# Four heads to a unit in the grouped-query layer of a cross-attention stack

## The chip, the core and the metric

The kernel runs on one core of a Trainium2 chip. TensorE (PE) multiplies matrices and writes to PSUM, which has eight banks of 512 fp32 columns on 128 partitions; VectorE (DVE), ScalarE (ACT) and GpSimd (POOL) do the rest, and SyncE (SP) issues most transfers between DRAM and on-chip memory. The engines run side by side, each through its own queue in order, and wait for each other on semaphores. The metric is the device time of one execution in microseconds (us); the time before is a median over runs, and the traces come from one further, profiled execution.

## The reference

Four attention layers transform `x` (2048 queries of 256 values) against one context of 1601 tokens of 512 values. Layers 0, 2 and 3 are alike: 16 heads of 64 values, with a bias of -20 times a mask on the columns of a few named tokens. Layer 1, the second one, is the subject here: 16 query heads of 16 values share four key and value heads, and `x` is normalized first.

```python
# masked layers (three of them)
logits = einsum('bhqd,bhkd->bhqk', q, k) * 64 ** -0.5 + col_bias
out = einsum('bhqk,bhkd->bhqd', softmax(logits), v)
x = out @ Wo + bo + x
# second layer
inv = rsqrt(mean(x * x, axis=-1) + 1e-5)
xn = x * inv * norm_w
q = (xn @ wq).reshape(B, T, 16, 16)       # query heads 4g .. 4g+3 belong to group g
k = (cond @ wk).reshape(B, S, 4, 16)
v = (cond @ wv).reshape(B, S, 4, 16)
scores = einsum('btgrd,bsgd->bgrts', qg, k) * 16 ** -0.5
x = x + einsum('bgrts,bsgd->btgrd', softmax(scores), v).reshape(B, T, 256) @ wo
```

## The kernel before

The queries are cut into four sets of 512 (`b`), the 1601 keys into 13 chunks of 128 (the last of 65). `x` stays on the chip, transposed, in `xs`. A *block* is a pair of heads of a masked layer, or a group of four query heads of the second. A *unit* is one set of queries with one pair of heads: 32 units for each masked layer (8 blocks, 4 sets), and 32 for the second layer (4 blocks, 4 sets, two pairs per group, the list `SUBS`).

One loop (L1052) writes the order of all work. A *step* handles one chunk of three units at once: the scores of one unit (`ca`), the exponentials of a unit 17 steps behind (13 chunks and `DELAY` 4) and the values of a unit one step further behind (`LAG` 1). The engines' orders are pinned to what this loop writes (L1107 to L1113), except that GpSimd and the transfers are not.

In a masked unit, `masked_scores` multiplies two heads on 64 partitions each in fp32 (L755), ScalarE copies the scores to SBUF (L767), and VectorE keeps a running maximum over the keys (L772). After 13 steps the maximum is transposed, reduced and spread over all partitions through DRAM (`maxima`, `on_all_partitions`, `maxima_spread`). Then VectorE subtracts it (L837), ScalarE takes the exponential (L844), GpSimd adds up the chunks for the denominators (L849), and PE multiplies by the values, two heads on 64 columns each (L872).

In a unit of the second layer, `split` has cut the 16 values of each query and key into three bf16 parts, and `stack` has laid eight products of parts along the 128 contraction rows (`q8`, `k8`); a ninth product lies apart (`k9`, `max_rows`). Row maxima come from one bf16 matmul per head with 512 keys (`grouped_scores`, L788), reduced by VectorE straight from PSUM (L793); the negated maxima are cut into three parts, transposed (L828) and copied into three rows of `max_rows` (L831). The input of the exponentials is computed by two more matmuls per head (L853 and L858), the second of which subtracts the maximum, and ScalarE takes the exponential from PSUM (L862). The values carry a column of ones, so that the denominators come out as a row of the result (`denominators`, L900).

What fills the gaps are *pieces*: projections of keys, values and queries, denominators, output projections. Each has a cost, and is written at the end of a step when its due step has come or when the step's credit allows it (`Pieces.step`). Most of them write the one PSUM bank `pm`. The other banks: two buffers of two banks for scores (`ps_s`), one buffer of two for the spread maxima of masked units (`ps_b`, which the second layer also uses for scores), and one bank for the values' result.

Before the second layer starts, `normalize` (L654) computes the root mean square of each set of queries with ones as weights, divides `x` by it on VectorE and stores the normalized `x` in DRAM; the keys of the second layer are projected and split chunk by chunk (`keys`, L524) during the last block of the first layer.

Of the kernel before, what the change touches and what calls it, by code (L numbers as in the profile page):

```python
# [18 lines left out]
P = 128  # L19
QB = 512  # L20
# [13 lines left out]
def tile_cross_attention_stack(ctx: ExitStack, tc: tile.TileContext, t: dict, out: bass.AP):  # L34
# [23 lines left out]

    nc = tc.nc
# [15 lines left out]
    NP = 19  # L75
# [7 lines left out]
    ps_s = ctx.enter_context(tc.tile_pool(name="ps_s", bufs=2, space=PSUM))  # L83
    ps_b = ctx.enter_context(tc.tile_pool(name="ps_b", bufs=1, space=PSUM))
# [6 lines left out]
    nc.vector.memset(ones, 1.0)  # L91

# [117 lines left out]
    def first_context_slice(i):  # L210
# [3 lines left out]
        for c in range(4 * i, min(4 * i + 4, NT)):  # L214
# [6 lines left out]
            pt = ps_s.tile([P, NCT, P], FP, name="s")  # L221
# [14 lines left out]
    MX, RA, RB, RE = 0, 3, 6, 9  # L236
    HALVES = (0, 64)
    max_keys = const.tile([P, P], BF, name="max_keys")
    tail_keys = [const.tile([P, NTAIL], BF, name=f"tail_keys{l}") for l in range(NL)]
    max_cols = const.tile([P, QT, P], FP, name="max_cols")  # L240
# [14 lines left out]
    def token_rows():  # L255
# [6 lines left out]
        nc.gpsimd.memset(max_cols, 0.0)  # L262
# [4 lines left out]
        row_of = small.tile([P, 3], FP, name="row_of", bufs=1)  # L267
        for j, (r0, r1) in enumerate(((MX, RA), (RA, RB), (RB, RE))):
            for h in HALVES:
                nc.vector.tensor_reduce(  # L270
                    row_of[h : h + 64, j : j + 1], ident[h : h + 64, h + r0 : h + r1], AX.X, ALU.add
                )
        for b in range(NB):
            for h in HALVES:
                nc.vector.tensor_copy(
                    max_cols[:, :, h + RA : h + RE],
                    parts[:, :, b * QT : (b + 1) * QT].rearrange("p r q -> p q r"),
                )
            pt = ps_m.tile([P, QT, P], FP, name="pm")
            for q in range(QT):  # L280
                nc.tensor.transpose(pt[:, q, :], max_cols[:, q, :], ident)
            nc.vector.tensor_copy(bias_rows[:, ts(b, QB)], pt.rearrange("p a b -> p (a b)"))
        nc.gpsimd.memset(max_cols, 0.0)
        nc.vector.memset(max_keys, 0.0)
        for h in HALVES:
            nc.vector.memset(max_keys[h : h + RA, :], 1.0)
        for l in range(NL):
# [3 lines left out]
            for to, j in ((0, 0), (1, 2)):  # L291
# [11 lines left out]
            nc.vector.tensor_scalar(tail_keys[l], only, row_of[:, 1:2], row_of[:, 0:1], ALU.mult, ALU.add)  # L303
            nc.vector.scalar_tensor_tensor(
                tail_keys[l], marks[:, 1, :], row_of[:, 2:3], tail_keys[l], ALU.mult, ALU.add
# [13 lines left out]
    den_rows = const.tile([P, 2], FP, name="den_rows")  # L319
    one_row = const.tile([P, 1], FP, name="one_row")  # L320
    nc.gpsimd.memset(one_row, 0.0)
    for h, r in enumerate(HALVES):
        nc.gpsimd.tensor_copy(den_rows[:, h : h + 1], ident[:, r + 16 : r + 17])
        nc.gpsimd.memset(one_row[r : r + RA, :], 1.0)
# [5 lines left out]
    class Masked:  # L330
# [25 lines left out]

        def wo(self, u, sub):
            return u.wo
# [34 lines left out]
        def query_pieces(self, unit):  # L393
# [4 lines left out]
            def queries(j):  # L398
                if j == 0:
                    unit.q = heads.tile([P, QB], FP, name="q")  # L400
# [10 lines left out]
    class Grouped:  # L411
# [3 lines left out]

        BLOCKS, HEADS = 4, 2
        SUBS = [(0, 1), (2, 3)]
        name = "L1_xattn_"
        OWN = 32
        ka = vs = None
        Q_PARTS = (0, 0, 0, 1, 1, 1, 2, 2)  # L430
        K_PARTS = (0, 1, 2, 0, 1, 2, 0, 1)

        def stackers(self, kind, parts):

            both = [const.tile([P, 4, 8, 16], BF, name=f"{kind}{x}") for x in "ab"]
            for x in both:
                nc.gpsimd.memset(x, 0.0)
            for j, part in enumerate(parts):
                half = 0 if part == 0 else 64
                nc.gpsimd.tensor_copy(  # L440
                    both[part // 2][:, :, j, :],
                    ident[:, half : half + 64].rearrange("p (h d) -> p h d", d=16),
                )
            return both

        def load(self, n):
# [3 lines left out]
            if n == 0:  # L450
                self.sel_q = self.stackers("sel_q", self.Q_PARTS)
                self.sel_k = self.stackers("sel_k", self.K_PARTS)
                self.last_q = const.tile([P, 2, P], BF, name="last_q")
                self.last_k = const.tile([P, 4, P], BF, name="last_k")
                nc.gpsimd.memset(self.last_q, 0.0)
                nc.gpsimd.memset(self.last_k, 0.0)
                for h, r in enumerate(HALVES):
                    to = slice(r + self.OWN, r + self.OWN + 16)
                    for i in range(2):
                        j = 64 + 16 * self.SUBS[i][h]  # L460
                        nc.gpsimd.tensor_copy(self.last_q[:, i, to], ident[:, j : j + 16])
                    for g in range(4):
                        j = 64 + 16 * g
                        nc.gpsimd.tensor_copy(self.last_k[:, g, to], ident[:, j : j + 16])
                self.wk = weights.tile([P, NCT, 2, 64], FP, name="wk", bufs=1)
                self.wv = weights.tile([P, NCT, 64], FP, name="wv", bufs=1)
                for half in range(2):
                    nc.sync.dma_start(
                        out=self.wk[:, :, half, :],
                        in_=t[self.name + "wk"].rearrange("(k p) f -> p k f", p=P),  # L470
                    )
                nc.sync.dma_start(
                    out=self.wv, in_=t[self.name + "wv"].rearrange("(k p) f -> p k f", p=P)
                )
            u.wq = weights.tile([P, NC, 2, 64], FP, name="wq")
            for half in range(2):
                nc.sync.dma_start(
                    out=u.wq[:, :, half, :],
                    in_=t[self.name + "wq"][:, ts(n, 64)].rearrange("(k p) f -> p k f", p=P),
                )  # L480
            return u

        def load_wo(self, u):
            u.wo_of = weights.tile([P, 2, C], FP, name="wo")
            nc.gpsimd.memset(u.wo_of, 0.0)
            for i in range(2):
                for h, r in enumerate(HALVES):
                    j = 64 * u.n + 16 * self.SUBS[i][h]
                    nc.sync.dma_start(
                        out=u.wo_of[r : r + 16, i, :], in_=t[self.name + "wo"][j : j + 16, :]  # L490
                    )

        def wo(self, u, sub):
            return u.wo_of[:, sub, :]

        def split(self, src, a, b, scale):

            top = slice(64, P)
            nc.scalar.mul(a, src, scale)
            rest = work.tile([P, 512], FP, name="rest", bufs=1)  # L500
            less = rest[top, : src.shape[1]]
            nc.vector.scalar_tensor_tensor(
                less, src[top], scale, a[top], ALU.mult, ALU.subtract
            )
            nc.vector.tensor_copy(a[top], less)
            nc.vector.tensor_tensor(b[top], less, a[top], ALU.subtract)

        def stack(self, dst, sel, j, a, b):
            n = a.shape[1]
            ps = ps_m.tile([P, 512], FP, name="pm")  # L510
            nc.tensor.matmul(
                ps[:, :n], sel[0][:, j].rearrange("p t d -> p (t d)"), a, start=True, stop=False
            )
            nc.tensor.matmul(
                ps[:, :n], sel[1][64:, j].rearrange("p t d -> p (t d)"), b[64:],
                start=False, stop=True,
            )
            nc.vector.tensor_copy(dst, ps[:, :n])

        def projections(self, u):  # L520
            if u.n:
                return None

            def keys(c, ct):  # L524
                if self.ka is None:
                    self.ka = heads.tile([P, T], BF, name="ka", bufs=1)
                    self.kb = heads.tile([P, T], BF, name="kb", bufs=1)
                a, m = TCH[c]
                pk = ps_m.tile([P, QB], FP, name="pm")[:, :m]
                for k in range(NCT):  # L530
                    nc.tensor.matmul(
                        pk, self.wk[:, k].rearrange("p h d -> p (h d)"), ct(k)[:, :m],
                        start=(k == 0), stop=(k == NCT - 1),
                    )
                self.split(pk, self.ka[:, a : a + m], self.kb[:, a : a + m], 1.0)
# [14 lines left out]
        def own_keys(self, u):  # L550


            def begin():
                u.kT = heads.tile([P, T], FP, name="kT")
                both = u.kT[:, :].bitcast(BF)
                u.k8, u.k9 = both[:, :T], both[:, T:]

            def stacked(a, n):
                if u.kT is None:
                    begin()  # L560
                self.stack(
                    u.k8[:, a : a + n], self.sel_k, u.n, self.ka[:, a : a + n],
                    self.kb[:, a : a + n],
                )

            def last(a, n):
                ps = ps_m.tile([P, 512], FP, name="pm")
                nc.tensor.matmul(
                    ps[:, :n], self.last_k[64:, u.n, :], self.kb[64:, a : a + n],
                    start=True, stop=True,  # L570
                )
                nc.scalar.activation(
                    u.k9[:, a : a + n], ps[:, :n], AF.Identity, bias=one_row
                )

            found = []
            for a, n in TBK:
# [569 lines left out]
```

## Time and profile before

| | us |
|---|---|
| median of 3 runs (5645.54 to 5646.53) | 5646.52 |
| the profiled execution | 5638.94 |
| its span, first to last instruction | 5637.2 |
| PE busy in the span | 5255.5 (93%) |
| VectorE busy | 3981.3 (71%) |
| ScalarE busy | 3346.0 (59%) |
| GpSimd busy | 3018.6 (54%) |
| first exponential of the second layer, from the span's start | 1582.3 |
| its last exponential | 2903.6 |

A line of the profile names the source line, the engine, the operation, and what is written from what (`s<-q,kT`) with partitions and columns; "x4" merges four records, and an fp32 matmul leaves two records, each with its own weight load (PEld). "Idle before" is how long the engine had waited, with what ended it. Of two successive lines on PE the difference of the starts is what the first one costs, since records overlap at their ends. The three masked layers lie before and behind the second one; the granted TensorE clock is a share of full speed.

### The profile page before, as it was taken

How to read it: one execution, taken by the hardware profiler on the slowest of the kernel's cores; microseconds unless marked ns; L12 is line 12 of the kernel's file. 1: busy time of each engine (PE TensorE's matmuls, PEld its weight loads, DVE VectorE, ACT ScalarE, POOL GpSimd, SP SyncE). 2: the span in 40 equal slices, each digit the busy share in tenths (PEclk: the TensorE clock that was granted, in tenths of full speed). 3: DMA queues.
4: the chain of work that ended last, by engine and by line, in shares of the span. 5: the costliest groups of instructions: out<-in, count | busy, mean ns of one | idle time of the engine just before them, and what ended most of it. 6: DMA issues, size and time to landing. Idle time of an engine off the chain costs nothing.

```text
span 5637.2 us, 63697 instructions
## 1 busy us (share of the span) xinstructions
PE 5255.5 (93%) x23412; PEld 2070.8 (37%) x23412; DVE 3981.3 (71%) x4183; ACT 3346.0 (59%) x4096; POOL 3018.6 (54%) x1476
## 2 busy tenths in 40 slices
PE   6899999998889999999999999999999999999997
PEld 4333433343322333233334334333334333334332
DVE  3777777778765555555557777777777777777786
ACT  2666666665533333333356667666667666667675
POOL 1677777775520000000026777777777777777777
PEclk8999999999889999999999999999999999999998
DMA  4222222222100000001112222222222222222211
GB/s 122 63 68 82 75 69 79 76 72 57 53 29 11 16 15 15 11 17 27 47 47 76 78 74 75 78 73 74 78 72 75 77 75 71 77 73 77 74 37 33
DMA packets 341864, 337.99 MB, mean 60 GB/s; under 512 B 110089, under 2 KB 295689, under 8 KB 341552
## 3 DMA queue, kind: packets, MB, share of 16 engines
q1 hardware_dynamic: 338288, 328.53, 20.6%
q8 instruction: 185, 3.03, 0.2%
q0 software_dynamic: 1152, 3.28, 0.2%
q10 hardware_dynamic: 2112, 2.10, 0.1%
q14 instruction: 127, 1.04, 0.1%
HBM read 319.16 MB, written 14.68 MB: 59 GB/s over the span
## 4 chain that ended last, share of the span: by engine, by line
PE 80%; DVE 9%; ACT 7%; issue 3%; DMA 1%; POOL 0%; SPq 0%; ACTq 0%; POOLq 0%; DVEq 0%; another core or an unknown queue 0%
PE po L872 24%; PE s L755 20%; PE pm L369 6%; PE pm L380 6%; PE pm L916 4%; PE pm L404 4%; ACT p L767 3%; DVE p L837 2%; PE s L853 2%; PE s L788 2%; PE s L809 2%; ACT p L844 2%; PE s L858 2%; DVE top L772 2%; PE pm L892 1%
## 5 line engine op out<-in xcount | busy, mean ns | idle before, releaser
L849 POOL TENSOR_TENSOR sums<-sums,p 128x1024 f32<-128x1024 f32 (+1 forms) x1152 | 2725.1, 2366 | 1089.6 <-ACT p L844 1012.1
L872 PE MATMUL po<-p,v 128*64 128x512 f32 (+1 forms) x6656 | 1813.3, 624 | 83.8 <-ACT p L844 44.3
L767 ACT COPY p<-s 128x1024 f32<-128x1024 f32 (+1 forms) x1248 | 1262.3, 1012 | 951.5 <-PE s L755 787.0
L772 DVE TENSOR_TENSOR top<-s,top 128x1024 f32<-128x1024 f32 (+1 forms) x1056 | 1291.6, 1223 | 680.4 <-ACT p L767 678.6
L837 DVE TENSOR_TENSOR p<-p,b 128x1024 f32<-128x1024 f32 (+1 forms) x1248 | 1506.5, 1208 | 72.8 <-ACT b L824 71.4
L844 ACT ACTIVATE p<-p 128x1024 f32<-128x1024 f32 (+1 forms) x1248 | 1322.0, 1059 | 169.5 <-DVE p L837 163.3
L755 PE MATMUL s<-q,kT 64*128 64x512 f32 (+1 forms) x4992 | 1414.9, 643 | 5.7 <-DVE top L772 3.6
L910 POOL TENSOR_TENSOR oT<-oT,by 128x512 f32<-128x512 f32 x128 | 163.8, 1280 | 1160.8 <-DMA by<-cols 901.1
L872 PEld LDWEIGHTS po<-p,v 128*64 128x64 f32 (+1 forms) x6656 | 331.5, 135 | 1076.7 <-issue 271.0
L862 ACT ACTIVATE p<-s 128x1024 f32<-128x1024 f32 (+1 forms) x283 | 289.4, 1023 | 439.1 <-PE s L858 439.1
L755 PEld LDWEIGHTS s<-q,kT 64*128 64x128 f32 (+1 forms) x4992 | 368.7, 182 | 450.4 <-issue 223.4
L793 DVE TENSOR_REDUCE row_top<-s 128x2 f32<-128x1024 f32 x261 | 319.0, 1224 | 153.3 <-PE s L788 152.0
L380 PE MATMUL pm<-wv,ct 128*128 128x128 f32 (+1 forms) x2392 | 344.4, 287 | 78.9 <-DVE rden L893 50.7
L380 PEld LDWEIGHTS pm<-wv,ct 128*128 128x128 f32 (+1 forms) x2392 | 286.6, 187 | 284.7 <-issue 142.0
L369 PE MATMUL pm<-ct,wk 128*128 128x128 f32 (+1 forms) x2392 | 346.0, 288 | 45.8 <-DVE rden L893 32.4
L369 PEld LDWEIGHTS pm<-ct,wk 128*128 128x128 f32 x2392 | 290.3, 191 | 258.3 <-issue 175.6
L916 PE MATMUL pm<-oT,wo 128*128 128x512 f32 x512 | 292.2, 653 | 13.3 <-POOL oT L910 12.5
L862 ACT ACTIVATE p<-b 128x1024 f32<-128x1024 f32 (+1 forms) x133 | 136.0, 1023 | 219.4 <-PE b L858 219.4
L922 DVE TENSOR_TENSOR xs<-pm,xs 128x512 f32<-128x512 f32 x232 | 158.3, 682 | 104.3 <-PE pm L916 104.3
L793 DVE TENSOR_REDUCE row_top<-b 128x2 f32<-128x1024 f32 x123 | 150.6, 1224 | 77.5 <-PE b L788 76.7
L383 ACT COPY v<-pm 128x128 f32<-128x128 f32 (+1 forms) x312 | 82.2, 264 | 186.8 <-PE pm L380 179.0
L847 POOL COPY sums<-p 128x1024 f32<-128x1024 f32 x96 | 99.5, 1037 | 170.6 <-ACT p L844 170.6
(187 smaller groups left out, 3451.3 us busy)
## 6 DMA issues: line engine op xcount, KB each, us to landing
ct<-ctxT SPq DMA_DIRECT2D x288, 512.0 KB, 4.0
xT<-xT SPq DMA_DIRECT2D x104, 512.0 KB, 3.5
spread<-cols SPq DMA_DIRECT2D x96, 512.0 KB, 3.7
by<-cols SPq DMA_DIRECT2D x256, 128.0 KB, 3.1
ct<-ctxT SPq DMA_DIRECT2D x48, 130.0 KB, 2.7
wk<-in_L_xattn_Wk_dram SPq DMA_DIRECT2D x24, 256.0 KB, 5.1
wv<-in_L_xattn_Wv_dram SPq DMA_DIRECT2D x24, 256.0 KB, 2.8
xT<-xs SPq DMA_DIRECT2D x12, 512.0 KB, 2.7
```

What stands on the lines that cost most here:

```text
L369: nc.tensor.matmul(pk, u.wk[:, k, :], ct(k)[:, :m], start=(k == 0), stop=(k == NCT - 1))
L380: nc.tensor.matmul(pv, ct(k)[:, :m], u.wv[:, k, :], start=(k == 0), stop=(k == NCT - 1))
L755: nc.tensor.matmul(s[:m, h, :], self.u.kT[r, a : a + m], self.q[r, :], start=True, stop=(a != TAIL),)
L767: nc.scalar.copy(p[:m], s[:m])
L772: nc.vector.tensor_tensor(self.top[:m], s[:m], self.top[:m], ALU.max)
L793: nc.vector.tensor_reduce(self.top[:, :, q, k : k + 1], s, AX.X, ALU.max)
L837: nc.vector.tensor_tensor(self.p[c][:m], self.p[c][:m], self.less[:m], ALU.add)
L844: nc.scalar.activation(p[:m], p[:m], AF.Exp)
L849: nc.gpsimd.tensor_tensor(self.sums[:m], self.sums[:m], p[:m], ALU.add)
L862: nc.scalar.activation(p[:m], s[:m], AF.Exp)
L872: nc.tensor.matmul(self.po[r, :], u.v[:m, c, r], self.p[c][:m, h, :], start=(c == 0), stop=(c == NT - 1),)
L916: nc.tensor.matmul(py, wo[:, ts(k, P)], self.oT, start=True, stop=True)
```

## The change

Four things change.

1. A unit of the second layer holds the four heads of a group (`SUBS = [(0, 1, 2, 3)]`), each on 32 partitions: 16 rows of queries or keys, and a seventeenth which holds the negated maximum (queries) and ones (keys). Scores are plain fp32 matmuls, 16 rows for the row maxima, 17 for the exponentials; splitting and stacking go. The values of each head go to 32 columns.
2. The normalization becomes a factor of the queries: `x` is stored as it is, `norm_w` goes into the query weights, and the inverse root (with the scale of the scores) is spread over the partitions through DRAM and multiplied into the projected queries. The negated maxima reach the seventeenth row through DRAM as well.
3. PSUM: six banks are handed out by a small class, least recently used first: in pairs to masked units, one by one to the second layer. A step of the second layer goes in two parts, each with two row maxima, two exponentials and the values of four heads over half the queries.
4. In the masked layers the denominators are transposed in one piece into a pair of score banks, two steps after the last values, and reduced once, instead of in two pieces of one head each through `pm`.

```diff
-    NP = 19
+    NP = 21
+    banks = ps_s.tile([P, 6, QB], FP, name="s")
+        def pair(self, of=(0, 2)):
+            i = min(of, key=lambda i: max(self.used.index(i), self.used.index(i + 1)))
+            self.take((i, i + 1))
+            return banks[:, i : i + 2, :]
+        def one(self, of):
+            i = next(i for i in self.used if i < of)
+            self.take((i,))
+            return banks[:, i, :]
...
+            u.wq = weights.tile([P, NC, 4, 32], FP, name="wq")
+            nc.gpsimd.memset(u.wq, 0.0)
...
+                nc.gpsimd.tensor_scalar(
+                    u.wq[:, k], u.wq[:, k], normw[:, k : k + 1], None, ALU.mult
+                )
...
-                self.split(pk, self.ka[:, a : a + m], self.kb[:, a : a + m], 1.0)
+                nc.scalar.copy(self.ks[:, a : a + m], pk)
...
+            def spread(a, n):
+                pk = ps_m.tile([P, QB], FP, name="pm")[:, :n]
                 nc.tensor.matmul(
+                    pk, sel[:, u.n].rearrange("p h d -> p (h d)"), self.ks[:, a : a + n],
                     start=True, stop=True,
                 )
+                nc.scalar.activation(u.kT[:, a : a + n], pk, AF.Identity, bias=one_row)
+            return [Piece(lambda a=a, n=n: spread(a, n), n / 512) for a, n in TBK]
...
+                nc.vector.tensor_tensor(unit.q[:, part], pq, factors[:, unit.b, part], ALU.mult)
...
-    def normalize(l, b):
+    def norm_factors(l, b):
...
+            pt = ps_m.tile([P, QT], FP, name="pm")
+            for q in range(QT):
+                for k in range(NC):
+                    nc.tensor.matmul(
+                        pt[:, q : q + 1], held["x"][:, k, columns(q)], ones[:, :1],
+                        start=(k == 0), stop=(k == NC - 1),
+                    )
+            by = small.tile([P, 1, QT], FP, name="factor")
+            nc.vector.tensor_scalar(by[:, 0, :], pt, 16.0 / C, 16.0 * EPS, ALU.mult, ALU.add)
+            nc.scalar.activation(by, by, AF.Sqrt)
             nc.vector.reciprocal(by, by)
+            on_all_partitions(by, [(factors[:, b, :], slice(0, 1))])
...
+        def row_maxima(self, i, h, s):
...
+                nc.tensor.matmul(
+                    s[:, at : at + n], self.q[r, columns(q)], self.u.kT[r, a : a + n],
+                    start=True, stop=True,
+                )
...
+                on_all_partitions(
+                    ntop,
+                    [(self.q[r + 16 : r + 17, :], slice(h, h + 1)) for h, r in enumerate(QUARTERS)],
+                )
...
+        def grouped_exp(self, c, h, s):
             a, m = TCH[c]
+            r = self.rows(h, 17)
+            nc.tensor.matmul(
+                s[:m], self.u.kT[r, a : a + m], self.q[r, :], start=True, stop=True
+            )
...
+            nc.scalar.activation(self.p[c][h // 2][:m, h % 2, :], s[:m], AF.Exp)
...
+                    at = ts(part, QB // 2)
+                    to, v = self.po[r, at], u.v[:m, c, :]
+                    p = self.p[c][h // 2][:m, h % 2, at]
...
-                pt = ps_m.tile([P, QT, P], FP, name="pm")
-                for q in range(QT):
-                    nc.tensor.transpose(pt[:, q, :], self.sums[:, h, columns(q)], ident)
-                nc.vector.tensor_reduce(rden[:, h, :], pt, AX.X, ALU.add)
+                pt = psum.pair().rearrange("p h (q k) -> p h q k", k=P)
+                for h in range(2):
+                    for q in range(QT):
+                        nc.tensor.transpose(pt[:, h, q, :], self.sums[:, h, columns(q)], ident)
+                nc.vector.tensor_reduce(rden, pt, AX.X, ALU.add)
...
+        for part in range(2):
+            for j in range(2):
+                if scoring and not scoring.masked:
+                    scoring.row_maxima(ca, 2 * (1 - part) + j, psum.one(singles))
+                if exping and not exping.masked:
+                    exping.grouped_exp(cb, 2 * part + j, psum.one(singles))
+            if valuing and not valuing.masked:
+                valuing.values(cv, part)
...
-            own = 6.0 if scoring.masked else 4.6
+            own = 6.0 if scoring.masked else 5.0
```

`columns(q)` is every fourth query from `q` on; `rows(h, n)` gives head `h` its 64 or 32 partitions, or the first `n` of them; `QUARTERS` are the partitions 0, 32, 64 and 96; `singles` is 6 in the second layer, and 4 while a masked unit is scored or exponentiated beside it.

## The prediction

> **What bounds the kernel now.** I read busy time by stage first, because the second layer is a different program from the other three. The columns are stretch, length, busy time (and instructions) of PE, weight loads, VectorE, ScalarE and GpSimd, granted clock, DMA share, GB/s.
>
> ```profile
> span 5637.2 us, 63697 instructions
> ```
> ```profile
> 1100.00:1250.00 150.00, 145.54 (x655) 58.88 (x652) 116.98 (x110) 104.04 (x129) 109.62 (x50) 1.00 0.28 77
> 1260.00:1580.00 320.00, 258.87 (x1024) 97.64 (x1024) 260.87 (x280) 170.33 (x207) 184.06 (x91) 0.88 0.19 52
> 1582.00:2907.00 1325.00, 1246.58 (x5437) 418.72 (x5437) 710.34 (x1006) 509.88 (x574) 50.83 (x57) 0.99 0.08 22
> 4000.00:4500.00 500.00, 482.29 (x2196) 198.49 (x2194) 389.23 (x364) 345.54 (x430) 360.63 (x166) 1.00 0.26 74
> ```
>
> TensorE is the bound at 94% in the second layer (1582 to 2907, from its first exponential to the first of the next layer) and at 96% in masked layers (4000 to 4500). VectorE has 54% and ScalarE 38% in the second layer: room for an exchange. From 1260 to 1580, where it is prepared, PE falls to 81% and VectorE equals it.
>
> Then a step in time order, the second layer's first, a masked one's second (start, busy us; successive starts give the cost):
>
> ```profile
> 2203.38 0.59 PE L788 MATMUL s<-kT,q 128*128 128x512 bf16 x2
> 2203.81 0.59 PE L853 MATMUL s<-q,kT 128*128 128x512 bf16 x2
> 2204.33 0.39 PE L858 MATMUL s<-max_rows,kT 64*128 64x512 bf16 x2
> 2204.65 1.08 PE L872 MATMUL po<-p,v 128*64 128x512 f32 x4
> 2205.67 0.60 PE L788 MATMUL b<-kT,q 128*128 128x512 bf16 x2
> ```
> ```profile
> 4292.62 1.13 PE L404 MATMUL pm<-xs,wq 128*128 128x256 f32 x4
> 4293.69 1.13 PE L755 MATMUL s<-q,kT 64*128 64x512 f32 x4
> 4294.74 1.08 PE L872 MATMUL po<-p,v 128*64 128x512 f32 x4
> 4295.75 1.16 PE L369 MATMUL pm<-ct,wk 128*128 128x128 f32 x8
> ...
> 4303.53 1.12 PE L916 MATMUL pm<-oT,wo 128*128 128x512 f32 x2
> 4304.58 1.08 PE L755 MATMUL s<-q,kT 64*65 64x512 f32 x4
> ```
>
> A grouped step costs 2.29 us for two heads (2203.38 to 2205.67), the fp32 values 1.02 of it. The second excerpt carries the forecast: one fp32 matmul of 512 columns on the whole array (L916, two records) takes 1.05 us from start to start, and so do two heads on 64 rows each (L755, four records) or on 64 columns each (L872, 1.01). Parts of the array work side by side. Four strips of 32 occur nowhere in this trace.
>
> **The change, part by part.**
>
> *Steps of the second layer.* 416 steps of two heads become 208 of four. A step has two parts, each with four fp32 score matmuls (two row maxima, two exponential inputs) on four row strips, then the values of four heads on four column strips over half the queries.
> - Scores of a part: if four strips overlap as two do, L755's 1.05. The maxima take every fourth query as weights; L900 loads such weights:
>
> ```profile
> L916 PEld LDWEIGHTS pm<-oT,wo 128*128 128x128 f32 x512 | 77.1, 190 | 223.1 <-issue 102.2 <-DVE p L837 69.7 <-DVE row_top L795 25.2
> L900 PEld LDWEIGHTS pm<-den_rows,oT 128*128 128x128 f32 x256 | 62.1, 327 | 26.8 <-issue 26.8
> L893 DVE TENSOR_REDUCE rden<-pm 128x4 f32<-128x512 f32 x192 | 130.8, 682 | 21.2 <-PE pm L892 21.2
> L878 ACT COPY oT<-po 128x512 f32<-128x512 f32 x128 | 73.2, 572 | 3.1 <-PE po L872 3.1
> ```
>   327 against 190 ns: +0.14 for the first load; the second lies under the first pass. 1.19.
> - Values: a 256-column fp32 matmul is half of L404's 1.07, and column strips overlap (L872): 0.54.
> - Banks: six are handed round, four per part, so a part's third matmul takes the bank of the previous part's first maximum. That one ends about 1.3 us after its part began (1.19 and some latency), its reduction takes 0.68 (L893) and the release some 0.05: 2.05 against 1.73. A wait also lengthens the part, so it settles at half the difference: 0.16. In PE's queue stand behind it the fourth score and the values, then VectorE and ScalarE.
>
> Part 1.89, step 3.8 us. VectorE needs 4×0.68 = 2.7 of it, ScalarE 4×0.57 = 2.3: both fit, without much room on VectorE. Bounds: 3.46 without the bank wait; the far upper ones are the rivals.
>
> *Per unit* of four heads: 13×3.8 = 49.4. The last step's maxima load eight small strided weights per head in a row (L900's eight took 1.9 us) instead of streaming 1.1, in each part: +1.6. Pieces: queries 2.1 (two at L404's price), denominators 1.9, projection 2.1, own keys 0.9 (three blocks at L755's price and a short one, shared by four units). Sum 58.0. The same sum for a unit of before is 13×2.29 + queries 1.1 + stacking 1.6 + transposed maxima 0.6 + denominators 1.9 + projection 2.1 + own keys 0.5, less 0.2 for the short last step: 37.4. The chip took 39.7: between 1700 and 2500 there are 262 exponentials, 13 per 39.7 us. I carry the 2.3 of stalls over: 60.3. Sixteen units are 965 us; 32×39.7 = 1270 of the 1325 leaves 55 for the first units and the third layer's first projections, of which I keep 40. New 1005, gain **320**.
>
> *What goes off the path at nothing.* The negated maxima now go through DRAM to row 16 of each head's queries: five more transfers on SP's queue per unit, the first behind VectorE's reduction. A cols store lands in 2.4 us and a by load in 3.1, with some 0.4 to issue each, about 8 us; exponentials begin four steps (15 us) later. Without that cover each us beyond 15 costs 16 us in all. The denominators' five transfers have the four steps ahead of the division. Weight padding on GpSimd has an almost idle engine (51 of 1325 us).
>
> *Preparation, 1260 to 1580.* VectorE loses the key and query splitting and the normalized x:
>
> ```profile
> L505 DVE CAST ka<-rest 64x128 bf16<-64x128 f32 (+1 forms) x13 | 19.2, 1475 | 0.4
> L677 DVE SCALAR_TENSOR_TENSOR xT<-xs,normw,rest 128x128 f32<-128x128 f32 x24 | 15.3, 679 | 0.4
> L675 DVE RECIPROCAL rest<-rest 128x128 f32<-128x128 f32 x12 | 11.3, 943 | 0.0
> ```
>   With the smaller ones (L502, L506, L518, L669, about 16) that is 62 us, and 13 come back (52 maxima of 0.68 for 18 of 1.22). PE gains 2 us per block of queries for eight strided weight loads of the norm. At the 42.4 us of an undisturbed masked unit the stretch would take 69 us less. I take **45**; ends 20 (PE, at 259 of 320, becomes the next bound) and 69.
>
> *Masked layers.* Two bursts of four transposes through the one pm bank become one of eight through a score pair. These waits on pm go (us, times):
>
> ```profile
>   PE pm L380: 50.7, 40
>   PE pm L369: 32.4, 24
> ```
>   83 us in 96 units, 0.87 each. What is late next: the following scores find the other pair. Its reader, VectorE's maximum, ends 3.5 us after its scores began (4293.69 to 4297.19), and PE is back after 1.05 + 1.01 + 1.16 = 3.2 us: a wait of 0.3. **55** gained; ends 100 (no new wait, one burst cheaper) and a loss of 45 (no gain, and waits of 0.5).
>
> *Sum.* The profiled execution took 5638.94 us, 1.7 outside its span. 5639 − 320 − 45 − 55 = 5219. The median of the runs shown is 0.13% above that execution: 5226.
>
> *A rule of the Trainium skill against the row.* L755 and L872 show two strips at full overlap. The Trainium skill, "TensorE: Matmul & The Clock Gate", section "Measured speedup vs the span model", gives 3.07× for four row strips and 2.38× for three column strips. By it, as an estimate, 0.26 and 0.11 us are added per part, of which 0.16 is the bank wait covered: 92 us more in all, 5318. I keep to the rows; no run here shows four strips.
>
> **The rivals.**
>
> *Only two strips overlap at a time.* Nothing here shows more than two. Scores of a part then take two rounds, 2.1 us, values 1.0: step 6.2, unit 91.5, the layer 1504, +179; with the other gains 5718, on the median 5725. Slower. It decides from a step of 5.8 us on. Against it: the two strips start within one record of each other, though each has two passes to run, so the second pass of a strip does not hold up the next strip.
>
> *Nothing of the four overlaps*: four whole matmuls per part, 4×1.05 + 4×0.54, step 12.7: far slower, about 7080.
>
> *VectorE sets the step.* If the third and fourth scores wait for both reductions, another 0.34 falls on each part, 208×0.68 = 141 us: 5367. For it: VectorE's share rises to some 75% and its queue also holds query scaling and additions to x. Against it: 2.7 of 3.8 us.
>
> *No new wait binds*: step 3.46 and the masked gain whole, 5226 − 71 − 45 = 5110.
>
> **How the numbers follow.** Forecast 0.62, VectorE 0.18, no wait 0.07, two strips 0.09, no overlap 0.04. The likeliest gives 5226 us. Low end 5090: the case without waits and 20 for the preparation's upper end. High end 5430: VectorE's case, the preparation's lower end and part of the masked loss; two strips and no overlap stay outside. A difference under 0.2% can't be told from none. Only the two-strip case can end near the present time, with little chance: faster 0.86, same 0.02, slower 0.12.
>
> **What would show it.** Four matmuls of a part starting within some 0.05 us and a part of 1.7 to 2.0 us; PE waits on the maxima of about 0.16 per part, waits of ScalarE on PE else; exponentials of the layer spanning about 1000 us; pm no longer waiting on the denominators, and a score wait of about 0.3 us once per masked unit instead; VectorE below 75% from 1260 to 1580. I am wrong if parts last 3 us (strips in pairs), if PE waits on maxima in every part for 0.5 us, or if the transfers to row 16 hold up the first exponentials.

## The result, and the profile after

The changed kernel takes 12158.23 us (median of 4 runs, 12155.27 to 12168.67) against 5646.52 (5645.54 to 5651.14): 2.153 times the time before, interval 2.150 to 2.157. The forecast was 5226 us. First the head of the changed kernel's page (busy time of each engine, and the granted clock in 40 slices):

```profile
span 12167.0 us, 66902 instructions
PE 9060.4 (74%) x25652; PEld 3075.2 (25%) x25652; DVE 3833.2 (32%) x3920; ACT 3381.0 (28%) x4432; POOL 2975.4 (24%) x1429
PEclk7888888755555555555555555888888888888887
```

No engine is as busy as TensorE was before (93%), so engines wait for each other; and the granted clock is half of full speed through the second layer and below full speed elsewhere. The time splits at the second layer's first and last exponential, found in the timelines (us):

| | up to the first | first to last | from the last to the end |
|---|---|---|---|
| before | 1582.3 | 1321.4 | 2733.5 |
| after | 2690.1 | 4859.5 | 4617.4 |
| difference | +1107.8 | +3538.1 | +1883.9 |

Nearly half of the loss, 2992 us, lies outside the layer that was rewritten. The busy times by stretch answer to those shown of before (same columns; preparation by the same times, the second layer, a masked stretch; the kernel is late, so what it does from 1260 to 1580 is first-layer work):

```profile
1260.00:1580.00 320.00, 220.57 (x824) 83.68 (x822) 148.43 (x134) 130.64 (x161) 135.97 (x62) 0.87 0.16 46
2690.00:7550.00 4860.00, 3937.43 (x7505) 1119.05 (x7504) 573.37 (x873) 541.79 (x910) 26.09 (x33) 0.51 0.02 5
9000.00:9500.00 500.00, 346.03 (x1298) 132.81 (x1298) 232.63 (x210) 206.31 (x255) 212.98 (x99) 0.87 0.16 45
```

In a masked stretch PE is busy 69% where it was 96%. The table of waits (who waited for what; us in total, times, longest) names what holds it:

```profile
PEld s L659 <- DVE p L732: 2375.1, 1151, 5.1
PEld s L747 <- DVE row_top L696: 1634.7, 704, 2.4
PEld s L691 <- ACT p L753: 1087.6, 659, 3.6
```

None of the three is a wait that the algorithm needs. L659 is a masked unit's scores and L732 the subtraction of another unit's maximum; L691 is a row maximum and L753 the exponential of another head. The timeline of the second layer shows them at work (start, length, engine, line, what; in brackets the idle time before and what ended it):

```profile
5000.07 2.09 PE L691 MATMUL s<-kT,q 16*128 16x512 f32 x2
5002.20 0.69 DVE L696 TENSOR_REDUCE row_top<-s 128x1 f32<-128x512 f32 x1 [5.20 <-PE s L691]
...
5002.95 2.07 PE L747 MATMUL s<-q,kT 17*128 17x512 f32 x2 [0.78 <-DVE row_top L696]
5005.06 0.60 ACT L753 ACTIVATE p<-s 128x512 f32<-128x512 f32 x1 [5.29 <-PE s L747]
...
5005.71 2.09 PE L691 MATMUL s<-kT,q 16*128 16x512 f32 x2 [0.69 <-ACT p L753]
5007.83 0.69 DVE L696 TENSOR_REDUCE row_top<-s 128x1 f32<-128x512 f32 x1 [4.93 <-PE s L691]
...
5010.58 1.08 PE L771 MATMUL po<-p,v 128*32 128x256 f32 x8
...
5011.59 2.09 PE L691 MATMUL s<-kT,q 16*128 16x512 f32 x2
```

Matmul, its reader, the next matmul, its reader: each score matmul but the first of a part, which follows the values, begins some 0.05 us after the reader of the one before it has ended, and it writes another bank. A part takes 11.52 us (5000.07 to 5011.59) where 1.89 were forecast; 26 parts to a unit are 300 us, sixteen units 4800 of the 4860. The masked units show the same (9000 to 9015):

```profile
9006.08 2.08 PE L659 MATMUL s<-q,kT 64*128 64x512 f32 x4
...
9008.25 1.01 ACT L671 COPY p<-s 128x1024 f32<-128x1024 f32 x1 [1.80 <-PE s L659]
...
9010.44 1.21 DVE L732 TENSOR_TENSOR p<-p,s 128x1024 f32<-128x1024 f32 x1
...
9011.70 1.13 PE L659 MATMUL s<-q,kT 64*128 64x512 f32 x4 [1.09 <-DVE p L732]
```

The scores at 9011.70 go to a pair of banks that nobody reads. They wait until the subtraction has ended (10.44 + 1.21 = 11.65), which reads the spread maxima in a third pair. A step takes 5.62 us here (9006.08 to 9011.70), so that a masked unit's 13 steps are 73 us; a unit took 42.4 us before.

### The profile page after: what moved, and what is told of

The parts are those of the page before. It is cut to its first block, busy times and chain, and to the rows that moved or that the text cites. A ratio compares the mean times of both kernels' runs of the same rounds, so it can differ in the third digit from the quotient of the medians.

```text
span 12167.0 us, 66902 instructions
## 1 busy us (share of the span) xinstructions
PE 9060.4 (74%) x25652; PEld 3075.2 (25%) x25652; DVE 3833.2 (32%) x3920; ACT 3381.0 (28%) x4432; POOL 2975.4 (24%) x1429
## 5 line engine op out<-in xcount | busy, mean ns | idle before, releaser
L659 PE MATMUL s<-q,kT 64*128 64x512 f32 (+1 forms) x4992 | 1735.4, 777 | 1771.5 <-DVE p L732 1749.4
L771 PE MATMUL po<-p,v 128*64 128x512 f32 (+3 forms) x8320 | 2196.6, 726 | 11.3 <-ACT p L737 8.4
L747 PE MATMUL s<-q,kT 17*128 17x512 f32 (+1 forms) x1664 | 1698.3, 1121 | 651.1 <-DVE row_top L696 552.1
L691 PE MATMUL s<-kT,q 16*128 16x512 f32 (+1 forms) x2048 | 1725.6, 962 | 309.2 <-ACT p L753 265.5
L753 ACT ACTIVATE p<-s 128x512 f32<-128x512 f32 (+1 forms) x832 | 496.5, 597 | 4171.7 <-PE s L747 4171.7
L696 DVE TENSOR_REDUCE row_top<-s 128x1 f32<-128x512 f32 x768 | 531.3, 692 | 3542.0 <-PE s L691 3542.0
L732 DVE TENSOR_TENSOR p<-p,s 128x1024 f32<-128x1024 f32 (+1 forms) x1248 | 1506.0, 1207 | 121.4 <-ACT s L727 109.4
L659 PEld LDWEIGHTS s<-q,kT 64*128 64x128 f32 (+1 forms) x4992 | 427.5, 210 | 2428.5 <-DVE p L732 2375.1
L691 PEld LDWEIGHTS s<-kT,q 16*128 16x128 f32 x2048 | 537.0, 316 | 1306.7 <-ACT p L753 1087.6
L747 PEld LDWEIGHTS s<-q,kT 17*128 17x128 f32 (+1 forms) x1664 | 395.5, 295 | 1831.9 <-DVE row_top L696 1634.7
L771 PEld LDWEIGHTS po<-p,v 128*64 128x64 f32 (+3 forms) x8320 | 376.4, 152 | 1766.9 <-issue 1698.2
L740 POOL COPY sums<-p 128x1024 f32<-128x1024 f32 x96 | 99.6, 1037 | 666.7 <-ACT p L737 666.7
```

What stands on the lines that cost most here:

```text
L659: nc.tensor.matmul(s[:m, h, :], self.u.kT[r, a : a + m], self.q[r, :], start=True, stop=(a != TAIL),)
L691: nc.tensor.matmul(s[:, at : at + n], self.q[r, columns(q)], self.u.kT[r, a : a + n], start=True, stop=True,)
L696: nc.vector.tensor_reduce(self.top[:, h, q, k : k + 1], s, AX.X, ALU.max)
L732: nc.vector.tensor_tensor(self.p[c][:m], self.p[c][:m], self.less[:m], ALU.add)
L747: nc.tensor.matmul(s[:m], self.u.kT[r, a : a + m], self.q[r, :], start=True, stop=True)
L771: nc.tensor.matmul(to, v, p, start=(c == 0 and not part), stop=(c == NT - 1 and part != 0))
```

## Experiments

Theory A: in these kernels a wait stands on a tile, not on a bank. The change makes one tile of six banks, so a matmul into any bank waits for the last reader of any other. The rival causes, as the expectations name them, lie in the array: that four strips (the 32 partitions which each head takes) do not overlap, that 16-row matmuls are slow in themselves, or that the low clock came first. Times of before are those of the runs on the same chip.

**Three tiles in place of one.** The changed kernel, with the six banks cut into three tiles of two:

```diff
-    banks = ps_s.tile([P, 6, QB], FP, name="s")
+    banks = [ps_s.tile([P, 2, QB], FP, name=f"s{i}") for i in range(3)]
-            return banks[:, i : i + 2, :]
+            return banks[i // 2]
-            return banks[:, i, :]
+            return banks[i // 2][:, i % 2, :]
```

> The changed kernel, with its one six-bank PSUM tile replaced by three tiles of two banks; nothing else. Theory A: the program's waits are kept per tile, so in the changed kernel each matmul into any of the six banks waits for the last reader of any other of them. Then a masked unit, whose pairs are now tiles of their own, goes back from 72 us to 42 or 43 (96 units, -2850 us), and the second layer, where a maximum and an exponential still share a tile, improves only in part: two pairs of the queue of matmul, reader, matmul, reader now overlap, from 310 us a unit to between 150 and 240. In all 6600 to 8200. Theory B: fp32 matmuls on four strips are slow in themselves or run one after another. Then masked units, which have no such strips, do not change (nothing in B explains their 72 us at all), and neither does the layer: about 12000.

8078.35 us (one run) against 5653.14, and 4080 less than with one tile. First exponential at 1627.7, last at 5392.4, 2684.2 after it: the stretches outside the second layer add up to 4312 us, against 4316 before, although the first exponential still comes 45 us late. The rest of the loss sits inside, where two matmuls of one tile still have two readers (from 3000 to 4000 the loads for the inputs of exponentials, L747, wait 475 us for the maxima's reductions). Busy times in the layer and behind it:

```profile
3000.00:4000.00 1000.00, 826.43 (x1930) 237.95 (x1932) 157.37 (x243) 134.77 (x226) 6.33 (x9) 0.51 0.01 4
6000.00:7000.00 1000.00, 981.64 (x4475) 403.74 (x4472) 792.16 (x721) 706.06 (x878) 736.85 (x336) 1.00 0.26 77
```

PE is back to 98% at a clock of 1.00 in masked units; in the layer it is at 83% and 0.51.

**The reverse: one tile for the kernel before.** Nothing of the change, but the buffers of the kernel before cut from one six-bank tile, handed round as they were:

```diff
+    banks = ps_one.tile([P, 6, QB], FP, name="s")
+            i = self.of[self.n % len(self.of)]
+            s = banks[:, i : i + 2, :]
...
+    ps_s, ps_b = Third((0, 2)), Third((4,))
```

> The kernel before, with nothing changed but its PSUM: the two score buffers and the third one are slices of one tile of six banks. Theory A: masked units go from 42 to about 72 us as in the changed kernel (+2850 in all), and the second layer's steps, bf16 as before, from 2.3 to about 4.5 us (+900): about 9400 in all. Theory B or any theory that blames the strips, the fp32 scores or the transfers of the maxima: no change, 5640 to 5700.

9315.83 us (one run) against 5653.14, with the same wait on top among PE's (L773 is the masked scores here, L855 the subtraction), and a masked stretch like that of the changed kernel:

```profile
PEld s L773 <- DVE p L855: 2379.3, 1148, 7.5
PE s L773 <- DVE p L855: 1778.1, 1044, 6.7
```
```profile
6000.00:6500.00 500.00, 346.63 (x1342) 133.04 (x1338) 238.90 (x222) 212.78 (x264) 218.51 (x101) 0.89 0.15 45
```

346.63 us of PE in 500 against 346.03: masked stretches lose as much as in the changed kernel, without any other part of the change. Outside the second layer this kernel takes 7057 us, the changed one 7308, the one before 4316: the one tile makes nearly all of that loss. The bf16 layer goes from 1321 to 2257 us. Theory A holds, in both directions.

**Pairs of heads with one reader.** The three tiles, and both matmuls into a tile have one reader, with one reduction or one exponential over 1024 columns; both maxima are issued ahead of both inputs of exponentials:

```diff
+            if scoring and not scoring.masked:
+                both = psum.pair(of_pairs)
+                for j in range(2):
+                    scoring.row_maxima(ca, 2 * (1 - part) + j, both)
+            if exping and not exping.masked:
+                both = psum.pair(of_pairs)
+                for j in range(2):
+                    exping.grouped_exp(cb, 2 * part + j, both)
...
+                nc.vector.tensor_reduce(self.top[:, two, q, k : k + 1], both, AX.X, ALU.max)
...
+                nc.scalar.activation(p[:m], both[:m], AF.Exp)
```

> The three tiles, and in the second layer the two matmuls that share a tile also share its reader: two row maxima go to one tile and are reduced by one instruction of 1024 elements, two exponentials to another, taken by one activation; of a part the maxima are written first. Theory A with strips that overlap as two do: the four matmuls of a part run together, the exponentials wait for the tile that VectorE's 1.22 us reduction of the part before holds, about 0.4 us per part: part 2.15, step 4.3, unit 67, layer about 1100, in all 5250 to 5450. Theory A with strips that overlap only in twos: step over 6, in all 5700 to 5850. Theory B, strips one after another: step over 12, in all 7000 or more.

5694.64 us (5687.93 to 5701.53) against 5653.14: ratio 1.008, interval 1.006 to 1.010. The waits are nearly gone (from 1700 to 2700 the loads for the scores wait 15 us for the maxima's reductions and 7 us for exponentials), and the kernel is still no faster than before. The layer takes 1467 us. The expectation failed: theory A with strips that overlap had 5250 to 5450, and the time lies just below the range of strips that overlap in twos. Busy times of a stretch in it, then one part on PE:

```profile
1800.00:2000.00 200.00, 199.22 (x988) 71.82 (x988) 71.78 (x68) 60.39 (x61) 3.81 (x7) 0.57 0.03 9
```
```profile
2106.22 1.24 PE L692 MATMUL s<-kT,q 16*128 16x512 f32 x2
...
2106.25 1.22 PE L752 MATMUL s<-q,kT 17*128 17x512 f32 x2
...
2107.26 1.06 PE L692 MATMUL s<-kT,q 16*128 16x512 f32 x2
2107.26 1.06 PE L752 MATMUL s<-q,kT 17*128 17x512 f32 x2
...
2108.26 1.08 PE L776 MATMUL po<-p,v 128*32 128x256 f32 x8
...
2109.27 1.24 PE L692 MATMUL s<-kT,q 16*128 16x512 f32 x2
```

It is not strips in twos: the four start within 0.03 us (four records on two lines). But both passes of all four take 2.04 us and the values 1.01, where 1.19 and 0.54 were forecast. PE is busy 99.6% of the stretch at a granted clock of 0.57: the second cause, which the waits had covered.

**Is it the rows in use?** A strip of 32 partitions holds 16 or 17 rows of data. The rows behind the seventeenth are zeros in both operands, and while the maxima are computed the seventeenth itself is ones in the keys but still zero in the queries. So the matmuls can take all 32 rows without changing a result:

```diff
-            r = self.rows(h, 16)
+            r = self.rows(h)
-            r = self.rows(h, 17)
+            r = self.rows(h)
```

> The kernel with three tiles and one reader each, in which the scores of the second layer take all 32 rows of a strip instead of 16 (maxima) and 17 (exponentials); the added rows hold zeros, so that nothing else changes. In the run without this edit PE was over 99% busy in the second layer, all four matmuls of a part started within 0.05 us, and the granted clock was 0.55 to 0.70. Theory P: the clock is granted by how much of the array works, and strips half filled count as half. Then it returns towards 1.0 here, a pass of 512 columns goes from 0.85 back to 0.43 us, a part to about 2.15 (with the wait on the tile that VectorE reduces) and the layer from 1470 to about 1100 us: 5300 to 5380 in all. Theory Q: the clock falls for another reason (four strips at once, strided weights, waits between the parts, zeros or not): no change, 5690, clock 0.6.

5349.32 us (5347.14 to 5352.42) against 5646.24: ratio 0.948, interval 0.946 to 0.949. The layer takes 1155 us in place of 1467, by two edits that add arithmetic on zeros. Preparation and layer by busy time, and the same two kinds of part:

```profile
1260.00:1580.00 320.00, 308.53 (x1448) 136.35 (x1446) 222.46 (x215) 172.08 (x203) 164.63 (x87) 0.89 0.21 56
1800.00:2000.00 200.00, 199.99 (x1348) 90.29 (x1344) 97.62 (x94) 78.95 (x80) 5.61 (x7) 0.93 0.06 14
```
```profile
2004.38 0.82 PE L692 MATMUL s<-kT,q 32*128 32x512 f32 x2
...
2004.56 0.70 PE L752 MATMUL s<-q,kT 32*128 32x512 f32 x2
...
2005.04 0.59 PE L692 MATMUL s<-kT,q 32*128 32x512 f32 x2
2005.09 0.59 PE L752 MATMUL s<-q,kT 32*128 32x512 f32 x2
...
2005.62 0.64 PE L776 MATMUL po<-p,v 128*32 128x256 f32 x8
...
2006.18 1.25 PE L692 MATMUL s<-kT,q 32*128 32x512 f32 x4
...
2007.03 0.30 PEld L752 LDWEIGHTS s<-q,kT 32*128 32x128 f32 x4 [0.30 <-DVE row_top L700]
2007.03 1.13 PE L752 MATMUL s<-q,kT 32*128 32x512 f32 x4
...
2008.09 0.64 PE L776 MATMUL po<-p,v 128*32 128x256 f32 x8
...
2010.62 1.24 PE L692 MATMUL s<-kT,q 32*128 32x512 f32 x2
```

Scores of a part now take 1.24 us (2004.38 to 2005.62) and values 0.56. Every other part is longer by 0.67 (2.47 from 2006.18 on, against 1.80), because the load for two of the four scores waits for the reduction (2007.03). At 2010.62 the passes last a whole us again, for a moment: the denominators' piece stands ahead of it.

**Half of it.** The kernel of one reader, with 32 rows for the maxima alone:

```diff
-            r = self.rows(h, 16)
+            r = self.rows(h)
```

> The same with 32 rows for the maxima alone; the exponentials stay at 17. Theory P: a clock and a time between the two, 5400 to 5600. Theory Q: 5690. If it is the rows of zeros that do not count, neither this nor the one with 32 rows everywhere moves.

5459.66 us (one run) against 5646.24; the layer takes 1262 us, between 1467 and 1155. In the same stretch:

```profile
1800.00:2000.00 200.00, 199.22 (x1215) 83.03 (x1214) 86.66 (x84) 73.50 (x76) 6.57 (x11) 0.81 0.05 11
```

With 66, 98 and 128 rows named by the four scores of a part, the clock is 0.57, 0.81 and 0.93, always with PE over 99% busy.

**32 rows in the changed kernel, one tile kept.** The same two edits on the kernel as changed:

```diff
-            r = self.rows(h, 16)
+            r = self.rows(h)
-            r = self.rows(h, 17)
+            r = self.rows(h)
```

> The changed kernel with its one tile of six banks as it is, and 32 rows for the scores of the second layer. If the clock follows the share of the array at work, a strip that runs alone (each matmul waits for the reader of the one before) is a quarter of it at best, and the clock stays at 0.5: 12000 to 12200. If full strips bring the clock back by themselves, the matmuls' 2.1 us halve and 3300 matmuls save about 1 us each: near 9000.

12168.18 us (one run) against 12158.23 without them, and the clock in the layer stays at 0.51. The waits still set the time, and where one strip runs at a time, 32 rows are a quarter of the array's 128. PE is busy only 81% here, so whether the rows or the gaps hold the clock down is not separated.

**The denominators' part alone**: the kernel before, with part 4 of the change.

```diff
-                pt = ps_m.tile([P, QT, P], FP, name="pm")
-                for q in range(QT):
-                    nc.tensor.transpose(pt[:, q, :], self.sums[:, h, columns(q)], ident)
-                nc.vector.tensor_reduce(rden[:, h, :], pt, AX.X, ALU.add)
+                pt = ps_s.tile([P, 2, QT, P], FP, name="s")
+                for h in range(2):
+                    for q in range(QT):
+                        nc.tensor.transpose(pt[:, h, q, :], self.sums[:, h, columns(q)], ident)
+                nc.vector.tensor_reduce(rden, pt, AX.X, ALU.add)
```

> The kernel before, with one part of the change alone: the denominators of the masked layers transposed in one piece into a score pair (its own rotating buffers) two steps after the last values. The forecast's own price for it was 55 us less, with ends of 100 less and 45 more: 5546 to 5690, 5590 likeliest. If waits on the score pair replace those on pm in full: 5646 within 0.2%.

5590.5 us (5585.09 to 5595.19) against 5653.14: 62.6 less, ratio 0.989, interval 0.987 to 0.990. The two waits of pm on L893 are gone, and this one comes in their place (besides it, the values wait for masked exponentials 62.6 us where it was 44.3):

```profile
PE s L755 <- DVE top L772: 27.5, 93, 1.9
```

0.30 us, once per masked unit (93 of 96).

**Towards a better version.** On the 32 rows: contiguous queries as weights, with the negated maxima stored in the order that this needs, by one transfer per head.

```diff
-                    s[:, at : at + n], self.q[r, columns(q)], self.u.kT[r, a : a + n],
+                    s[:, at : at + n], self.q[r, ts(q, P)], self.u.kT[r, a : a + n],
...
+                        out=rows[h].rearrange("a b -> (a b)").rearrange("(q p) -> p q", p=P),
```

> The version with 32 rows, with 128 queries in a row as the weights of the maxima instead of every fourth query; the negated maxima are stored accordingly, by four transfers with 4-byte elements in the place of one. By the forecast's term for strided weights (0.14 us per part, 416 parts) 58 us less, and about 1 us less per unit in the last step, where eight such loads per head follow each other: 5270 to 5300. If the loads are hidden by the wait on VectorE's tile: no more than 20 us less. If the four longer transfers reach row 16 late: slower than without.

5267.62 us (5259.47 to 5273.85) against 5650.96: ratio 0.933, interval 0.931 to 0.934. The layer takes 1070 us, 85 less, at a clock of 0.98. A part that waits, and the start of the next one (L699 maxima, L760 inputs of exponentials, L784 values):

```profile
2004.06 1.13 PE L699 MATMUL s<-kT,q 32*128 32x512 f32 x4
2004.95 1.13 PE L760 MATMUL s<-q,kT 32*128 32x512 f32 x4
2006.01 0.64 PE L784 MATMUL po<-p,v 128*32 128x256 f32 x8
2006.58 0.70 PE L699 MATMUL s<-kT,q 32*128 32x512 f32 x2
```

On top of it, the exponentials' matmuls are issued ahead of the maxima's in each part:

```diff
-            if scoring and not scoring.masked:
-                both = psum.pair(of_pairs)
-                for j in range(2):
-                    scoring.row_maxima(ca, 2 * (1 - part) + j, both)
             if exping and not exping.masked:
...
+            if scoring and not scoring.masked:
+                both = psum.pair(of_pairs)
+                for j in range(2):
+                    scoring.row_maxima(ca, 2 * (1 - part) + j, both)
```

> The same, and a part writes the exponentials' tile ahead of the maxima's, so that the third tile in turn is released by ScalarE (1.02 us) instead of VectorE (1.22 us). By the sum of the wait, half of the difference falls on each part: 0.1 us times 416 parts, 40 us less than without this edit, 5230 to 5260. If PE is no longer waiting there: the same as without.

5191.07 us (5187.0 to 5196.32) against 5650.96: ratio 0.919, interval 0.917 to 0.920. This beats both kernels, by 8.1% the one before. The layer takes 1001 us, and the kernel 77 less than without this edit, where 40 were expected. The layer in busy time, and the first kind of part again (same lines of the program):

```profile
1800.00:2000.00 200.00, 200.00 (x1578) 76.38 (x1578) 114.59 (x109) 95.49 (x97) 6.26 (x10) 0.98 0.07 14
```
```profile
2004.42 0.70 PE L760 MATMUL s<-q,kT 32*128 32x512 f32 x2
...
2004.44 0.70 PE L699 MATMUL s<-kT,q 32*128 32x512 f32 x2
...
2005.49 0.64 PE L784 MATMUL po<-p,v 128*32 128x256 f32 x8
...
2006.06 1.13 PE L760 MATMUL s<-q,kT 32*128 32x512 f32 x4
...
2006.67 0.30 PEld L699 LDWEIGHTS s<-kT,q 32*128 32x128 f32 x4 [0.31 <-ACT p L766]
2006.67 1.13 PE L699 MATMUL s<-kT,q 32*128 32x512 f32 x4
```

Scores of four heads take 1.07 us (2004.42 to 2005.49), values 0.57; in the next part two of the four scores start 0.61 late, behind ScalarE, where they started 0.89 late behind VectorE (2004.06 to 2004.95 above).

## Why the prediction was wrong, and where it was right

**The step that failed** is *Banks*: "six are handed round, four per part, so a part's third matmul takes the bank of the previous part's first maximum". It read the hand-out in `one()` and `pair()` as what sets the waits, and took banks for independent. They are slices of one tile, and the third matmul waited for the second one's reader, whatever its bank. The 0.16 us of this term became 11.52 − 3.05 = 8.5 us per part (3.05 being the part of the one-reader kernel, 2106.22 to 2109.27, nearly without these waits; the clock is 0.50 in both excerpts). Outside the second layer, where the masked pairs were costed as if they were separate too, 2992 us were lost where 100 were to be gained (45 in the preparation, 55 in masked layers). The line `ps_s.tile([P, 6, QB])` stood in the diff; the profile of before showed neither reading at work, since there each buffer was its own tile. The list of what would prove the forecast wrong had waits on maxima "in every part for 0.5 us", so the kind of wait was in view, but bounded by one reduction, and not seen to reach the masked layers.

**The second miss** is in *Scores of a part* and *Values*: 1.05 and 0.54 were taken from rows at a clock of 1.00, with 128 rows in use. With scores on 66 rows the same work took 2.04 and 1.01. The forecast had no term for the clock and no rival named it. So the first miss is not all of the error: the one-reader kernel, the nearest run without it, took 5695 us and not 5226. The Trainium skill, "TensorE: Matmul & The Clock Gate", section "What's actually happening", has the gate follow how busy PE has been. Here the busy share does not tell the clock: the second layer has 0.57 at 99.6% busy, and the masked stretch of the kernel before with one tile 0.89 at 69%, with whole-array matmuls.

**Strips.** Right: four overlap fully, so the rival of two strips at a time and that of no overlap fall. Where the clock is 1.00, scores take 1.07 (forecast 1.05, and 1.19 with strided weights, where 1.24 was measured), values 0.56 to 0.57 (0.54). By the rates of the same page's section "Measured speedup vs the span model", an estimate is 0.26 and 0.11 more; the runs have 0.02 and 0.03, and the measurement decides. (The 92 us that the forecast made of it are 87 by its own terms: 0.26 + 0.11 − 0.16 over 416 parts.)

**VectorE sets the step.** Not what happened: it is busy 57% of the stretch shown of the layer in the best version. But reductions do hold two scores of every other part by 0.67 us in the version with 32 rows, 0.33 per part. That lies between the forecast's 0.16 and this rival's 0.50 (another 0.34 on top). The engine is idle for half of the time; it holds PE up because three pairs go round and a part takes two.

**Strided weights.** The forecast's terms were 0.14 in each of 416 parts, 58 us, and 1.6 in each of 16 units, 26 us: 84. Contiguous weights gave 5349.32 − 5267.62 = 82. That the sums agree is partly luck. In the excerpts, scores of a part that does not wait fell from 1.24 to 1.07 us (2006.58 to 2007.65 in the contiguous version), but those of a part that waits did not fall (1.91, 2006.18 to 2008.09, against 1.95, 2004.06 to 2006.01), and part of the gain came with the clock, 0.93 to 0.98, for which the forecast had no term.

**Preparation.** The first exponential comes 69.5 us earlier with 32 rows (1512.8 against 1582.3), 17.7 of them by the denominators alone (1564.6): 52 against the forecast's 45. VectorE has 222 of 320 us from 1260 to 1580, 70%, where the forecast said below 75%; but the last 67 us of that stretch now belong to the layer. In the 320 us that end at 1510 it has 247, 77%, so this sign holds by the shift alone. PE, at 308 in either stretch, is the next bound that the forecast named.

**Masked denominators.** Right: −62.6 against −55, and the 0.3 us of wait on the scores was met at 0.30.

**Transfers to the seventeenth row.** Right in the versions run here: among the waits of the one-reader kernel none of the scores is on them, and the longest wait that names one is 0.8 us, once.

In the best version the stretches differ from before by −73.6, −320.8 and −53.9 us; the forecast's gain in the layer was 320. It is met, but with edits that the change did not have, and the equality is luck: without its 84 us for strided weights the forecast's own sum would have been 404, of which the waits, 0.30 us per part (0.61 in every other one) where 0.16 were forecast, took some 60.

## What to carry to other kernels

Buffers that are to be written and read at different times belong in tiles of their own: one tile cut into slices carries one wait for all, and it reaches every stage that shares it, including those the change does not touch. Give two operations that share a tile one reader. When work on TensorE is packed into strips, read the granted clock beside busy time, and where several strips run at once, fill a strip's rows with zeros rather than leave them out.

## What the hardware showed

- The granted clock went with the share of the array's rows in use, at equal busy time: 0.57, 0.81 and 0.93 for 66, 98 and 128 rows per part, and 0.51 with one strip at a time at 81% busy. That rows were the lever, and that rows of zeros count, is shown by edits that do nothing else.
- These figures are means over time, not speeds in between. Read in windows of 0.5 us, from 2000 to 2095, the clock is 0.50 or 1.00 in all but a few: 155 windows at 0.50 and 33 at 1.00 with 66 rows, 48 and 137 with 98 rows, 19 and 167 with 128 rows.
- The rule behind it is not shown: whether rows or rows times columns are counted, and over which time, stays open. So does why the clock still falls behind the denominators' piece (eight loads of 128 rows for four columns each): one spell at 0.50 of 3.4 us, from 2010.3 to 2013.8, in the version with 32 rows.
- Contiguous weights raised the clock too, from 0.93 to 0.98.
- Four strips of 32 rows overlap without loss in fp32, two passes each: 1.07 us for eight records at a clock of 1.00, where one strip alone at 0.50 takes 2.09 for two.
- Not tried: six tiles of one bank each, which would have left the change's order of work as it is (masked units read two banks at once).
